# Layer 0 of a two-layer macaron block: two VectorE steps moved to GpSimd and ScalarE

## The chip, the cores and the metric

One core of a Trainium2 chip runs the whole program. The metric is the device time of one execution in microseconds (us). Engines are called by their short names: PE is TensorE (PEld its weight loads), DVE is VectorE, ACT is ScalarE, POOL is GpSimd, SP is SyncE, which issues most of the DMAs. Matrix products land in PSUM, a small memory of eight banks per partition that PE, DVE and ACT use; the kernel keeps everything else in SBUF.

## The reference

The input x is 16 sequences of 512 tokens of width 128. Two layers follow each other, each as "half an FFN, attention, half an FFN". The change touches layer 0 only:

```python
x = x + 0.5 * ffn(layernorm(x))          # FFN with fp4-quantized inputs
x = x + attn(layernorm(x))               # 16 heads of width 8, relative positions
x = x + 0.5 * ffn(layernorm(x))
# ffn:
gate = fp4_linear(x, w_gate); y = fp4_linear(x, w_up)
h = silu(gate) * y
return fp4_linear(h, w_down)
# attn:
score = q @ k + q . pe_k[dist]           # dist = clip(j - i, -64, 64) + 64
attn = softmax(score)
ctx = attn @ v + attn . pe_v[dist]
return ctx @ W_out + b_out
```

`fp4_quant_dequant` takes blocks of 16 numbers, divides by their largest magnitude over 6, rounds to a grid of eight values and multiplies back. `pe_v[dist]` differs from a constant only in a band of 64 on either side of the diagonal. Layer 1 (linear attention, and an ordinary attention with a mixture of experts) is not changed.

## The kernel before, in words

Layer 0 works through 16 sequences `b`, each in two halves of 256 queries, so 32 units. For each unit there are these streams of work, each a Python generator that yields between steps:

- `maxima` (L332) computes the scores in tiles of 128 keys by 512 columns on PE (L263, and L267 where the tile lies in the band), and DVE takes the maximum of each tile (L341).
- `main` (L358) computes the same scores once more, ACT takes the exponential (L369), PE multiplies with V into the averages `av`, and with the band's table into `rps`. ACT copies the band's result into `RV` (L403); SP writes `RV` to DRAM (L406) and reads it back in another layout into `cr` (four DMAs, L409). ACT copies the averages from PSUM into `cx` (L412).
- `fin` (L416) adds the band part `cr` to the averages `cx` (L422, two instructions a unit), transposes `cx` on PE (L430), divides (L433, L434), and multiplies with the output matrix.
- `F.half` (L107) is half an FFN for 256 tokens: layer norm (with a power on POOL, L59), quantization (DVE L70 to L78, POOL L79 and L81), transposes, and then for each `j` of two blocks of 128 tokens: PE makes the gate `g` (L121), ACT its tanh (L122), DVE forms `(tanh+1)*g` (L123), PE makes the 'up' `u` (L125), DVE multiplies the two (L126). Then the product is quantized, transposed, and multiplied with `w_down` (L139). It runs twice for each half sequence: as `head` before the attention, as `tail` behind it. That makes 128 blocks `j` in all.
- `prep` and `prepV` make q, k and v of a coming sequence.

`interleave` (L446) merges the generators by due times; in `layer0` a unit's `fin` is due from 0.45 of a unit after `main` ends, its `tail` after `fin`, and the `head` of three sequences later in the same unit. The order in which Python traces the instructions gives their priorities. From these and its own durations, the framework's planner lays out the order of the instructions on each engine ahead of time: an engine takes the instruction that the plan has ready first. On the chip each engine then runs its list strictly in that order, and waits where an input is late. Two devices bend the plan: `high_priority` (L341), and `issue_after(a.last)` in `fin` (L425), which keeps the add L422 behind the latest score maximum that was traced, in DVE's list.

Buffers that matter: PSUM tiles `mps` come from a pool of two (`pM`), shared by FFN, `prep` and `fin`; score tiles `sps` from a pool of three (`pS`), shared by `maxima` and `main`. The FFN's SBUF pool `fk` has two buffers of each name: `f_h`, `q_y`, `q_M` and so on. `cr` and `cx` have one buffer each.

Of the kernel before, what the change touches and what calls it, by code (L numbers as in the profile page):

```python
# [8 lines left out]
F32 = mybir.dt.float32  # L9
# [3 lines left out]
AF = mybir.ActivationFunctionType  # L13
ALU = mybir.AluOpType
# [3 lines left out]
I = 352  # L18
# [65 lines left out]
class FFN:  # L84
# [22 lines left out]
    def half(f, xb, half, wk, pp):  # L107

        s=f.s; nc=s.nc
        xh=xb[:,2*half:2*half+2,:]  # L110
        xn=wk.tile([128,2,128],F32,name="f_x")
        yield from s.ln_steps(xh,xn,wk,2)
        for xq in s.quant_steps(xn.rearrange("p a b -> p (a b)"),wk,128,16,"xq"): yield
        ps=pp.tile([128,512],F32,name="mps")
        for j in range(2): nc.tensor.transpose(ps[:,j*128:(j+1)*128],xq[:,j*128:(j+1)*128],s.ident)
        xqT=wk.tile([128,256],F32,name="f_x"); nc.scalar.copy(xqT,ps[:,:256]); yield
        h=wk.tile([128,2,I],F32,name="f_h")
        for j in range(2):
            t=h[:,j,:]
            g=pp.tile([128,512],F32,name="mps")  # L120
            nc.tensor.matmul(g[:,:I],xqT[:,j*128:(j+1)*128],f.wguT[:,0,:],start=True,stop=True)  # L121
            nc.scalar.activation(t,g[:,:I],AF.Tanh,scale=0.5)  # L122
            nc.vector.scalar_tensor_tensor(t,t,1.0,g[:,:I],ALU.add,ALU.mult); yield  # L123
            u=pp.tile([128,512],F32,name="mps")
            nc.tensor.matmul(u[:,:I],xqT[:,j*128:(j+1)*128],f.wguT[:,1,:],start=True,stop=True)  # L125
            nc.vector.scalar_tensor_tensor(t,u[:,:I],0.5,t,ALU.mult,ALU.mult); yield  # L126
        for hq in s.quant_steps(h.rearrange("p a b -> p (a b)"),wk,128,44,"hq"): yield
        hq=hq.rearrange("p (a b) -> p a b",a=2)
        for j in range(2):
            ps=pp.tile([128,512],F32,name="mps")  # L130
            for c in range(3):
                P=min(128,I-c*128)
                nc.tensor.transpose(ps[:P,c*128:(c+1)*128],hq[:,j,c*128:c*128+P],s.ident)
            hT=wk.tile([128,3,128],F32,name="hT",bufs=1)
            nc.scalar.copy(hT[:,0:2,:],ps[:,:256])
            nc.scalar.copy(hT[:96,2,:],ps[:96,256:384])  # L136
            for c in range(3):
                P=min(128,I-c*128)
                nc.tensor.matmul(ps[:,384:512],hT[:P,c,:],f.wdT[:P,c,:],start=(c==0),stop=(c==2),skip_group_check=True)  # L139
            nc.vector.scalar_tensor_tensor(xh[:,j,:],ps[:,384:512],0.5,xh[:,j,:],ALU.mult,ALU.add); yield  # L140
# [5 lines left out]
class Attn0:  # L146
# [103 lines left out]
    @staticmethod  # L250
    def vers(kt,half):

        return 1 if kt*128+192<half*256+256 else 0
# [3 lines left out]
    def scores(a, out, kt, half, b, BD, TQ, KS):  # L257

        nc=a.nc; blk=half*8+b
        sd=a.side(kt,blk); ib=a.inband(kt,blk)  # L260
        o4=out.rearrange("p (x g c) -> p g x c",x=8,g=4)
        for g in range(4):
            nc.tensor.matmul(o4[:,g],KS[:,sd,g*512+kt*128:g*512+(kt+1)*128],BD[:,g,:,b*32:b*32+32].rearrange("p h (x j) -> p x h j",j=4),start=(g==0),stop=(not ib and g==3),skip_group_check=True)  # L263
        if ib:
            for x in range(8):
                w0=kt*128-blk*32-x+a.OFF
                nc.tensor.matmul(out[:,x*64:x*64+64],a.ET[:,w0:w0+128],TQ[:,:,b*32+4*x:b*32+4*x+4],start=False,stop=(x==7),skip_group_check=True)  # L267
# [57 lines left out]
    def load(a, b, half):  # L325
        nc=a.nc; i=b%2
        u=(2*b+half)%3; BD=a.BD[u]; TQ=a.TQ[u]; QS=a.QS[i]
        for j in range(4):
            nc.sync.dma_start(BD[j*32:j*32+29,:,j,:],QS.rearrange("(g j) r q -> j r g q",j=4)[j][:,:,half*256:half*256+256])
            (nc.sync if b else nc.scalar).dma_start(TQ[j*32:j*32+24],a.QM[i][j][:,:,half*256:half*256+256].rearrange("h r q -> r h q"))  # L330
# [85 lines left out]
    def fin(a, b, half, X, wk, pM):  # L416

        s=a.s; nc=a.nc; cx,cr=a.pend.pop((b,half)); xb=X[b]
        def add():
            for s2 in range(2):  # L420
                o=cx.rearrange("p z (b j s x) -> p s (z b) x j",j=4,s=2,x=4)[:,s2]
                nc.vector.tensor_tensor(o,o,cr.rearrange("p (x j z b s) -> p s (z b) x j",x=4,j=4,z=4,s=2)[:,s2],ALU.add)  # L422
        if a.last is None: add()
        else:
            with s.tc.issue_after(a.last): add()  # L425
        yield
        cn=wk.tile([128,2,128],F32,name="cn")
        for t in range(2):
            ps=pM.tile([128,512],F32,name="mps")
            for z in range(4): nc.tensor.transpose(ps[:,z*128:z*128+128],cx[:,z,t*128:t*128+128],a.ident)  # L430
            p3=ps.rearrange("p (h c) -> p h c",c=32)
            rc=wk.tile([128,16],F32,name="rc")
            nc.vector.reciprocal(rc,p3[:,:,8])  # L433
            nc.vector.tensor_tensor(cn[:,t,:].rearrange("p (h d) -> p h d",d=8),p3[:,:,0:8],rc.unsqueeze(2).to_broadcast([128,16,8]),ALU.mult)  # L434
            yield
        ps=pM.tile([128,512],F32,name="mps")
        for t in range(2): nc.tensor.transpose(ps[:,t*128:t*128+128],cn[:,t,:],a.ident)
        ct=wk.tile([128,2,128],F32,name="cn").rearrange("p a b -> p (a b)"); nc.scalar.copy(ct,ps[:,:256])
        ps=pM.tile([128,512],F32,name="mps")
        for t in range(2): nc.tensor.matmul(ps[:,t*128:(t+1)*128],ct[:,t*128:(t+1)*128],a.wo,start=True,stop=True)  # L440
        xh=xb[:,2*half:2*half+2,:]
        nc.gpsimd.tensor_tensor(xh,xh,a.bo.unsqueeze(1).to_broadcast([128,2,128]),ALU.add)
        nc.vector.tensor_tensor(xh,xh,ps[:,:256].rearrange("p (a b) -> p a b",a=2),ALU.add)
        yield
# [593 lines left out]
```

## Time and profile before

| what | value |
| --- | --- |
| runs | 3627.19, 3630.62, 3651.11 us; median 3630.62 |
| the profiled execution | 3633.94 us, its span 3632.2 us |
| layer 0 | from the start to about 2050 us; steady from 300 to 1950 |
| busy over the span | PE 78%, DVE 67%, ACT 47%, POOL 23% |
| L126: 'up' times gate, DVE | 128 instructions, 64.6 us |
| L422: band part added, DVE | 64 instructions, 68.4 us |

The profile shows one execution. A group of instructions is given with its count, its busy time in us and the mean of one in ns; then the idle time of the engine just before, with what ended it. A window line gives the busy time of each engine in a stretch of the span, with the count of instructions. The line of tenths cuts the span into 40 slices of 90.8 us. A list of waits has us in total, how often, and the longest.

### The profile page before, as it was taken

Reading aid. Unit: us, or ns where it says so; the run is one execution under the profiler, and the core shown is the slowest. Engines: PE = TensorE matmul, PEld = TensorE weight load, DVE = VectorE, ACT = ScalarE, POOL = GpSimd, SP = SyncE. Lnnn points to the kernel's source line nnn. Section 1 sums busy time; section 2 is a strip of 40 time slices with the busy share of each in tenths; the row PEclk is TensorE's granted clock in tenths of the full one; section 3 lists DMA queues with packets and bytes.
Section 4 is the critical chain, followed back from the end, with each engine's and each line's share of the span. In section 5 each row is a group of like instructions: output and inputs, shape, how many; then the busy total and the mean of one; then the engine's idle time right before and its main releaser. Section 6 shows DMA issues by size and latency. Waiting matters only on the chain. (4 is left out here: it accounts for less than half of the span.)

```text
span 3632.2 us, 95259 instructions
## 1 busy us (share of the span) xinstructions
PE 2825.0 (78%) x40077; PEld 2032.3 (56%) x40077; DVE 2444.9 (67%) x6508; ACT 1693.8 (47%) x3391; POOL 838.9 (23%) x789
## 2 busy tenths in 40 slices
PE   5578989889898889888896388873788888878570
PEld 3357777667676677666775244431565555555230
DVE  5568788777887788877773467774546655655356
ACT  3145555545455454545554155533455454445242
POOL 4122222222222222222110222212112211111226
PEclk8799999999999999999998599886899989989785
DMA  3232222321223222222210111104312222121401
GB/s 105 54 91 71 57 53 59 81 63 52 65 65 77 64 50 58 76 74 62 53 33 19 32 33 36 36 33 123 90 54 73 59 63 56 36 62 36 126 17 46
DMA packets 290159, 217.23 MB, mean 60 GB/s; under 512 B 77402, under 2 KB 257476, under 8 KB 289604
## 3 DMA queue, kind: packets, MB, share of 16 engines
q1 hardware_dynamic: 284468, 207.72, 21.6%
q8 instruction: 315, 5.16, 0.6%
q10 hardware_dynamic: 5264, 3.43, 0.4%
q14 instruction: 112, 0.92, 0.1%
HBM read 110.28 MB, written 100.78 MB: 58 GB/s over the span
## 5 line engine op out<-in xcount | busy, mean ns | idle before, releaser
L341 DVE TRANSPOSE_TENSOR_REDUCE mx<-sps 128x16 f32<-128x512 f32 x1024 | 702.5, 701 | 261.7 <-PE sps L263 137.2
L263 PE MATMUL sps<-a_BD,a_KS 128*128 128x128 f16 x8192 | 736.4, 222 | 136.2 <-DVE mx L341 65.6
L369 ACT ACTIVATE PT<-sps 128x512 f32<-128x512 f32 x1024 | 576.4, 599 | 433.8 <-PE sps L267 238.1
L263 PEld LDWEIGHTS <-a_KS 128*128 128x128 f16 x8192 | 546.1, 98 | 296.4 <-issue 260.0
L59 POOL TENSOR_TENSOR ln_rs<-ln_ve,negh 128x4 f32<-128x4 f32 (+1 forms) x192 | 176.9, 930 | 855.1 <-DVE ln_ve L58 760.6
L267 PE MATMUL sps<-a_TQ,a_ET 128*128 128x64 f16 x7168 | 370.3, 195 | 0.0
L721 DVE SCALAR_TENSOR_TENSOR moe<-mps,oh,moe 128x128 f32<-128x128 f32 x896 | 289.8, 341 | 110.7 <-PE mps L719 96.5
L79 POOL TENSOR_TENSOR q_M<-q_y,q_M 128x704 f32<-128x704 f32 (+2 forms) x129 | 157.0, 1218 | 784.6 <-DVE q_y L78 658.6
L719 PE MATMUL mps<-f_W,T 128*128 128x512 f32 x512 | 297.1, 701 | 24.8 <-DVE moe L721 20.0
L267 PEld LDWEIGHTS <-a_ET 128*128 128x128 f16 x7168 | 311.2, 99 | 2.3 <-issue 1.9
L274 PE MATMUL av<-PT,a_V 128*32 128x256 f32 x3840 | 251.9, 387 | 0.0
L894 DVE TENSOR_TENSOR a_at<-pp,a_cm 128x1024 f32<-128x1024 f32 x128 | 154.3, 1214 | 79.6 <-PE pp L892 78.6
L892 PE MATMUL pp<-a_F 64*128 64x128 f32 x2048 | 169.8, 306 | 41.4 <-DVE a_at L894 30.2
L892 PEld LDWEIGHTS pp<-a_F 64*128 64x128 f32 x2048 | 143.3, 206 | 93.0 <-DVE a_at L894 36.9
L719 PEld LDWEIGHTS mps<-f_W,T 128*128 128x128 f32 x512 | 102.7, 222 | 125.0 <-issue 75.3
L274 PEld LDWEIGHTS av<-PT,a_V 128*32 128x32 f32 x3840 | 121.4, 111 | 68.7 <-issue 5.0
L874 ACT ACTIVATE a_F<-pp 128x1024 f32<-128x1024 f32 x128 | 127.0, 1025 | 46.8 <-PE pp L872 40.5
L62 ACT ACTIVATE xn<-xn,ln_mr,ln_rs 128x128 f32<-128x128 f32 x256 | 103.6, 481 | 95.5 <-DVE ln_mr L60 75.2
L274 PE MATMUL rps<-PT,a_TV 128*32 128x64 f32 x6912 | 134.5, 222 | 4.6 <-issue 4.4
L139 PE MATMUL mps<-wdT,hT 128*128 128x128 f32 (+1 forms) x768 | 126.9, 301 | 5.6 <-ACT hT L136 4.0
L673 ACT COPY f_PT<-St 32x512 f32<-32x512 f32 x128 | 78.7, 615 | 106.0 <-DVE St L672 99.9
L872 PE MATMUL pp<-a_QK,a_PK 128*128 128x512 f16 x256 | 82.7, 413 | 54.4 <-DMA a_QK<-a1d 26.6
(342 smaller groups left out, 5330.2 us busy)
## 6 DMA issues: line engine op xcount, KB each, us to landing
QM<-a_HM SPq DMA_DIRECT2D x180, 128.0 KB
a_TQ<-QM SPq DMA_DIRECT2D x120, 192.0 KB
RD<-RV SPq DMA_DIRECT2D x32, 512.0 KB
a_KS<-KSd SPq DMA_DIRECT2D x128, 96.0 KB
a_QK<-a1d SPq DMA_DIRECT2D x128, 96.0 KB
xn<-X SPq DMA_DIRECT2D x32, 256.0 KB
a1d<-a_hi SPq DMA_DIRECT2D x64, 128.0 KB
a_BD<-QS SPq DMA_DIRECT2D x128, 58.0 KB
```

The lines of the kernel that those rows point to most:

```text
L59: nc.gpsimd.tensor_tensor(rs,ve,s.negh[:,:n],ALU.pow); yield
L79: nc.gpsimd.tensor_tensor(M[:P],y[:P],M[:P],ALU.subtract)
L263: nc.tensor.matmul(o4[:,g],KS[:,sd,g*512+kt*128:g*512+(kt+1)*128],BD[:,g,:,b*32:b*32+32].rearrange("p h (x j) -> p x h j",j=4),start=(g==0 ...
L267: nc.tensor.matmul(out[:,x*64:x*64+64],a.ET[:,w0:w0+128],TQ[:,:,b*32+4*x:b*32+4*x+4],start=False,stop=(x==7),skip_group_check=True)
L274: for p,q in mms[1:]: a.nc.tensor.matmul(*p,**q)
L341: with a.s.tc.high_priority(): r=nc.vector.tensor_reduce(mx[:,kt,:,bb],ps.rearrange("p (i c) -> p i c",c=32),axis=AX.X,op=ALU.max,apply_tr ...
L369: nc.scalar.activation(pt[:,:,bb*32:bb*32+32].rearrange("p h (x j) -> p x h j",j=4),ps.rearrange("p (x h j) -> p x h j",x=8,j=4),AF.Exp)
L719: nc.tensor.matmul(ps,yT[:,j*128:(j+1)*128],a.W[:,e2*4:e2*4+4,:],start=True,stop=True)
L721: nc.vector.scalar_tensor_tensor(moe[:,j,:],ps[:,e*128:(e+1)*128],oh[:,j,e2*4+e:e2*4+e+1],moe[:,j,:],ALU.mult,ALU.add)
L874: nc.scalar.activation(f,ps,AF.Relu)
L892: nc.tensor.matmul(ps[:,hh,bs],f[hh*64:hh*64+64,1,bs],f[hh*64:hh*64+64,0,bs],start=True,stop=True)
L894: nc.vector.tensor_tensor(k,ps.rearrange("p h (b q) -> p (h b) q",b=4),a.cm.unsqueeze(1).to_broadcast([128,8,128]),ALU.mult)
```

## The change

Two edits in layer 0. In the FFN, ACT copies `u` from PSUM into an SBUF tile `v`, with the factor 0.5, and POOL multiplies `t` by `v`; DVE did both in one instruction. The tile `v` takes a buffer of the name `q_y`, which the quantization uses as well. In `fin` the two adds go to POOL, and the order behind `a.last` is dropped.

```diff
@@ FFN.half
             nc.vector.scalar_tensor_tensor(t,t,1.0,g[:,:I],ALU.add,ALU.mult); yield
             u=pp.tile([128,512],F32,name="mps")
             nc.tensor.matmul(u[:,:I],xqT[:,j*128:(j+1)*128],f.wguT[:,1,:],start=True,stop=True)
-            nc.vector.scalar_tensor_tensor(t,u[:,:I],0.5,t,ALU.mult,ALU.mult); yield
+            v=wk.tile([128,704],F32,name="q_y")[:,:I]; nc.scalar.activation(v,u[:,:I],AF.Copy,scale=0.5); nc.gpsimd.tensor_tensor(t,t,v,ALU.mult); yield
@@ Attn0.fin
         def add():
             for s2 in range(2):
                 o=cx.rearrange("p z (b j s x) -> p s (z b) x j",j=4,s=2,x=4)[:,s2]
-                nc.vector.tensor_tensor(o,o,cr.rearrange("p (x j z b s) -> p s (z b) x j",x=4,j=4,z=4,s=2)[:,s2],ALU.add)
-        if a.last is None: add()
-        else:
-            with s.tc.issue_after(a.last): add()
+                nc.gpsimd.tensor_tensor(o,o,cr.rearrange("p (x j z b s) -> p s (z b) x j",x=4,j=4,z=4,s=2)[:,s2],ALU.add)
+        add()
         yield
```

## Prediction

> **What bounds the kernel now.** I read the page's tenths first, then stages of the span, then short windows inside layer 0, then the waits, then the groups by shape. The change touches layer 0 alone, which ends near 2050 us, so the shares of the whole span say little.
>
> ```profile
> PE   5578989889898889888896388873788888878570
> DVE  5568788777887788877773467774546655655356
> POOL 4122222222222222222110222212112211111226
> ```
>
> Slices 4 to 21 are layer 0's steady part: PE at 80 to 90%, DVE at 70 to 80%, POOL at 20%. By stages (PE, PEld, DVE, ACT, POOL busy, then clock, DMA share and GB/s):
>
> ```profile
> 300.00:1950.00 1650.00, 1455.67 (x26315) 1152.24 (x26308) 1282.15 (x2837) 841.24 (x1845) 366.65 (x344) 0.97 0.24 61
> 1950.00:2050.00 100.00, 51.20 (x672) 35.69 (x670) 41.89 (x108) 25.70 (x61) 23.79 (x28) 0.69 0.07 16
> ```
>
> No engine is full there: PE 88%, DVE 78%, ACT 51%, POOL 22%. Windows of 4 us show that the average hides two regimes:
>
> ```profile
> 1020.00:1024.00 4.00, 4.00 (x126) 2.94 (x119) 1.38 (x3) 2.90 (x8) 0.00 (x0) 1.00 0.16 37
> 1032.00:1036.00 4.00, 2.65 (x27) 1.32 (x24) 4.00 (x11) 1.55 (x3) 0.00 (x0) 1.00 0.57 155
> 1044.00:1048.00 4.00, 2.16 (x67) 1.62 (x55) 4.00 (x11) 1.41 (x6) 0.39 (x1) 1.00 0.24 45
> 1088.00:1092.00 4.00, 2.25 (x25) 1.97 (x27) 3.97 (x9) 1.47 (x3) 2.54 (x2) 1.00 0.00 0
> ```
>
> In the first, PE is full and DVE idles; in the others DVE is full and PE stands a third to half of the time. So DVE sets the pace in part of each unit. Cut into 4 us windows, 300 to 1950 us has 243 windows (972 us) with DVE 80% busy or more. PE idles 134.6 us in them (14%), and 60 us (9%) in the other 680. The waits say the same:
>
> ```profile
> PE sps L263 <- DVE mx L341: 48.9, 68, 3.9
> PE sps L263 <- ACT PT L369: 33.0, 77, 2.6
> PE mps L430 <- DVE cx L422: 12.5, 4, 9.9
> PE mps L133 <- POOL q_M L81: 4.5, 11, 0.9
> DVE ln_st L55 <- DMA x<-in_L_attn_x_dram: 45.5, 11, 5.2
> POOL qklo L144 <- DMA QS<-qklo: 84.8, 8, 13.4
> ```
>
> PE waits for DVE most, for ACT second, for POOL hardly. The last two lines are needed for a rival: transfers land later than the plan has them.
>
> **The change part by part.** Groups by shape:
>
> ```profile
> L422 DVE TENSOR_TENSOR cx<-cx,a_cr 128x512 f32<-128x512 f32 x64 | 68.4, 1119 | 20.7 <-DMA a_cr<-RD 20.7
> L126 DVE SCALAR_TENSOR_TENSOR f_h<-mps,f_h 128x352 f32<-128x352 f32 x128 | 64.6, 504 | 5.9 <-PE mps L125 5.4
> L99 ACT COPY wguT<-mps 128x352 f32<-128x352 f32 x2 | 0.8, 456 | 1.2 <-PE mps L98 1.2
> L79 POOL TENSOR_TENSOR q_M<-q_y,q_M 128x256 f32<-128x256 f32 x64 | 46.5, 727 | 150.7 <-DVE q_y L78 137.8 <-PE sps L263 10.2 <-DMA a_BD<-QS 1.4
> L669 POOL TENSOR_TENSOR S<-S,src 128x512 f32<-128x512 f32 x32 | 33.5, 1047 | 170.4 <-DVE src L668 122.3 <-ACT a_xT L830 44.1 <-DVE lg L701 1.5
> L298 POOL COPY a_HM<-qklo 128x512 f16<-128x512 f16 x16 | 27.9, 1744 | 1.0
> ```
>
> *Taken off DVE.* 133 us in all; the windows of L126 and L422 alone put 53.3 + 64.2 = 117.4 us of it between 300 and 1950, and 100.8 us of that in the 243 packed windows.
>
> *Given back by blocking.* A DVE instruction can stand behind POOL:
>
> ```profile
> 1080.16 0.18 DVE L71 TENSOR_SCALAR hq_sc<-hq_sc 128x44 f32<-128x44 f32 x1
> 1089.23 1.39 POOL L81 TENSOR_TENSOR q_M<-q_M,hq_sc 128x704 f32<-128x704 f32 x1
> 1089.68 0.98 DVE L71 TENSOR_SCALAR hq_sc<-hq_sc 128x44 f32<-128x44 f32 x1
> ```
>
> The same L71 took 0.18 us alone and 0.98 us when it began under L81. Over 300 to 1950, DVE instructions that overlapped POOL took some 40 us more than the medians of their forms without overlap; POOL was busy 367 us, so 0.11 us per us. New POOL work there: 106 products of 0.95 us (between L79's 727 ns for 256 columns and 1704 for 704, by columns) and 60 adds. The add reads and writes in steps of 32 and 256 bytes, which no POOL tensor_tensor here does. Its bounds: 1.05 us (L669, 512 columns contiguous) and 3.6 us (L687's 1267 ns times 1744/612, the strided copy L298 over the contiguous copy L902). I take L298's 1.74, the one strided row with 512 columns. That is 101 + 104 = 205 us, and 0.11 times it is 22 us back on DVE. Net relief 95 us, in the packed windows 0.84 of it: 80. Bounds: 0 and 45 us (double) back.
>
> The Trainium skill, SBUF — State Buffer, § Who interferes with whom, says that POOL shares a port pair with DVE as an exclusive lock: whichever starts first blocks the other for its whole instruction, if the DVE one has two SBUF inputs or runs in a two-port mode. By that rule L126, whose one input is PSUM, never met POOL, and its replacement does; L71's two rows agree. Were each of the 166 new POOL instructions to block one DVE instruction for half of itself, the sum would have 103 us back instead of 22, and the gain would be gone.
>
> The GPSIMD Engine Reference, § 7, says that reading SBUF with steps over 8 bytes costs about half more per element. With L687's 1.27 us that makes an estimate of 1.9 us an add, 122 us for 64 against my 111; no run here shows it, and § 4.1 of that page advises against elementwise work on this engine at all.
>
> *What the relief is worth.* Were the packed windows to fall to the others' 8.8% PE idle, they would shorten by x with 134.6 - x = 0.088 (972 - x), so x = 54. That is what taking all 100.8 us away could return before PE binds; I take 54 * 80/101 = **-42 us**. Ends: 0 and -80.
>
> *ACT's copies.* 128 of 0.456 us (L99, same shape): 58 us, ACT from 51% to 54% of the stretch. Each stands in ACT's list among the exponentials L369, and has to wait for PE's L125 and for a free `q_y` buffer; behind it stand L369, and PE waits for those through three `sps` buffers. ACT cost PE 33.0 us in 841 us of work; 50 us more make +2, and as much twice over for the waits at the head of its list: **+6**. Ends: 0 and +35 (doubling that row). `u`'s `mps` buffer is now freed by ACT instead of DVE, at about the same length, so no term.
>
> *POOL's results.* PE's L430 and DVE's L70 now wait for POOL. In POOL's list the products and adds stand in front of L59, L79, L81, L144 and L442. Nearest row: PE lost 4.5 us to 53 results of L81, 0.085 each; 106 products and 30 adds at that make **+12**. Ends: 0, and 5 us a unit (two adds of 3.6 in place of 1.12, all seen by PE) for 30 units, +150. Between the read of `cr` (L409) and DVE's add lie 8 to 22 us in the trace, which cover a longer add; if the planner moves L430 up, that cover goes.
>
> *Start and end.* Where nothing lies beside it (first heads, last two tails), a block pays 0.46 + 0.95 - 0.50 = 0.9 us and one more handover; six such blocks, 5 us, and the last add 2 * (1.74 - 1.12) = 1.2: **+7** with rounding up. Ends +2 and +15.
>
> *Nothing:* no DMA is moved or added; SP's list is as before, and `cr` is read again 40 us or more after the add. Layer 1 is untouched.
>
> Sum: -42 + 6 + 12 + 7 = -17 us on the profiled 3633.9, so **3617 us**. That execution lies 3.3 us above the median.
>
> **The rivals.**
>
> *Slower: POOL stands at the head of its list for `cr`.* Without the order behind `a.last`, the plan puts the add where it has `cr` landed; POOL is idle then and will take it at once. For: loads land later than planned (DVE waited 45.5/11 = 4.1 us for x each time, POOL 10.6 us for QS). While POOL stands, L79, L81, L59 and the new products stand behind it, DVE's L70 and L60 wait for those, and PE for DVE. Price: 4.1 us a unit, 30 units, 123 us; three quarters seen by PE, 92. In place of the +12: 3634 - 42 + 6 + 7 + 92 = 3697. It decides (over 1% slower) from 2.2 us a unit on. Against: DVE's add itself waited for `cr` only twice.
>
> *Faster: DVE sets the packed stretches alone.* The net relief comes through whole: 3634 - 80 + 6 + 7 = 3567. For: PE's biggest wait is on DVE. Against: PE's 88%.
>
> *The relief does nothing:* PE and DVE only trade places in the wait for each other, and the costs stay: 3634 + 25 = 3659.
>
> **How the numbers follow.** Forecast 0.33 (own range 3590 to 3650), slower rival 0.30, faster 0.23, no relief 0.14. One per cent, about what a measurement of this kernel can tell from no change, is 36 us: below 3594 lie the faster rival and 0.04 of the forecast, 0.27; above 3667 the slower rival and 0.05 of the no-relief case, 0.35; 0.38 between. The range takes in both rivals' values: 3560 to 3715, with some 0.1 left out on each side.
>
> **What would show it.** DVE in 300 to 1950 from 78% to 72%, POOL to 35%; the packed windows fewer. Adds of 1.74 us, products of 0.95, copies of 0.46. Small DVE instructions (L58, L60, L71) lengthened more often. Slower rival: POOL's wait for `a_cr<-RD` appears at 2 us a unit or more, and PE or DVE waits for POOL lines. What would make it wrong: an add over 3 us, ACT waiting long for a `q_y` buffer, or a new order of the whole plan.

## The result and the profile after

| | before | after |
| --- | --- | --- |
| median of the runs | 3632.1 us (3627.2 to 3651.1) | 3983.9 us (3977.2 to 3995.3) |
| span of the profiled execution | 3632.2 us | 3993.6 us |
| mean granted TensorE clock | 0.900 | 0.861 |

The ratio is 1.096, 95% interval 1.091 to 1.101: slower by 352 us, outside the range. Line numbers behind the adds of `fin` are lower by 2 in the kernel after (L430 is L428 there, L475 is L473). Units are counted from 0, so an odd unit is the second half of a sequence.

To see where the time went I cut each span at the end of the second L412 of a unit (its averages are copied), and at the last L140. A pair is two units, one sequence. "x" is DVE's idle time at L55 in the waits of over 1.5 us for x; "cr" is the idle time ahead of the adds L422 in all.

| us | start to unit 2 | unit 2 to 24 (a pair) | 24 to 31 | rest of layer 0 | layer 1 | x | cr |
| --- | --- | --- | --- | --- | --- | --- | --- |
| before | 364.3 | 1273.1 (115.7) | 342.0 | 65.6 | 1587.4 | 45.5 | 20.7 |
| after | 384.8 | 1557.1 (141.6) | 396.3 | 70.0 | 1585.4 | 75.9 | 466.3 |

Layer 1 is as before; the loss is 26 us in every pair, and more where the pipeline fills and drains. The page's tenths of after (slices of 99.8 us):

```profile
PE   5677787778778778777877755888278887887661
DVE  5566576567657557655755524777555665555446
POOL 5223223223323322322321122222211211111135
```

PE is at 70 to 80% where it was at 80 to 90%, DVE at 50 to 70%, and POOL at 20 to 30%: no engine is nearer its limit, all stand more. The window that holds about the same 26,300 matmuls as 300 to 1950 did before is now 2000 us long:

```profile
300.00:2300.00 2000.00, 1535.60 (x26293) 1205.92 (x26285) 1246.83 (x2678) 881.18 (x1948) 587.97 (x511) 0.88 0.20 50
```

The groups of the new work:

```profile
L422 POOL TENSOR_TENSOR cx<-cx,a_cr 128x512 f32<-128x512 f32 x64 | 128.0, 2037 | 466.3 <-DMA a_cr<-RD 442.0 <-ACT PT L369 19.9 <-ACT hT L136 4.5
L126 POOL TENSOR_TENSOR f_h<-f_h,q_y 128x352 f32<-128x352 f32 x128 | 124.3, 971 | 393.4 <-ACT q_y L126 339.7 <-DVE f_h L123 37.4 <-DVE mx L341 15.9
L126 ACT ACTIVATE q_y<-mps 128x352 f32<-128x352 f32 x128 | 59.6, 466 | 100.1 <-PE mps L125 92.7 <-POOL q_M L79 3.3 <-POOL ln_rs L59 0.2
```

An add takes 2.04 us (1.74 taken), a product 0.97 (0.95), a copy 0.466 (0.456): the durations were nearly right. What was not is the 442 us that POOL stands ahead of the adds for `cr`. The waits between 300 and 2300 show who stands with it:

```profile
POOL cx L422 <- DMA a_cr<-RD: 408.7, 23, 31.7
DVE ln_mr L60 <- POOL ln_rs L59: 195.4, 48, 18.0
PE sps L263 <- DVE mx L341: 155.2, 86, 15.5
PE mps L115 <- POOL q_M L81: 144.8, 10, 17.5
DVE ln_st L55 <- DMA x<-in_L_attn_x_dram: 75.9, 11, 9.3
PE mps L428 <- POOL cx L422: 50.7, 5, 18.5
```

In the steady part of before, PE's wait for DVE's L341 was 48.9 us, PE's for L81 4.5 us (at L133), and DVE's for L59 next to nothing:

```profile
DVE ln_mr L60 <- POOL ln_rs L59: 1.7, 4, 0.9
```

One odd unit of after (unit 11) shows the chain. Timeline of POOL: start, duration, and in brackets the idle time before with what ended it.

```profile
1005.88 1.38 POOL L59 TENSOR_TENSOR ln_rs<-ln_ve,negh 128x2 f32<-128x2 f32 x2 [14.00 <-DVE ln_ve L58]
1032.04 3.88 POOL L422 TENSOR_TENSOR cx<-cx,a_cr 128x512 f32<-128x512 f32 x2 [24.78 <-DMA a_cr<-RD]
1035.87 0.72 POOL L79 TENSOR_TENSOR q_M<-q_y,q_M 128x256 f32<-128x256 f32 x1
1036.55 1.02 POOL L59 TENSOR_TENSOR ln_rs<-ln_ve,negh 128x4 f32<-128x4 f32 x1
```

POOL is free at 1007.3, and the next instruction in its list is the add, for which `cr` lands at 1032. Behind it stands an L59 that only now can run; DVE has stood for that one:

```profile
1037.60 0.68 DVE L60 SCALAR_TENSOR_TENSOR ln_mr<-ln_mv,ln_rs 128x4 f32<-128x4 f32 x1 [14.54 <-POOL ln_rs L59]
```

SP's own list in the same place. `stream` has `loads` fetch the tables from which the next unit's scores are made: the keys into `a_KS` (L315, once in two units), the queries into `a_BD` and `a_TQ` (L329, L330, four each). The last copy into `RV` (ACT, L403) ends at 1011.1; its write to `RD` is issued at 1018.4, 7 us later, behind the last of these loads in SP's list, and the read back into `cr` 9.5 us after that:

```profile
1014.92 3.41 SPq L330 DMA_DIRECT2D a_TQ<-QM  x1
1018.43 0.72 SPq L406 DMA_DIRECT2D RD<-RV  x1
1027.98 1.37 SPq L409 DMA_DIRECT2D a_cr<-RD  x4
```

And windows of 4 us, columns as in the prediction:

```profile
1020.00:1024.00 4.00, 3.90 (x70) 2.62 (x68) 2.04 (x3) 1.73 (x4) 0.00 (x0) 1.00 0.25 74
1024.00:1028.00 4.00, 0.83 (x16) 0.65 (x12) 0.00 (x0) 0.00 (x0) 0.00 (x0) 0.95 0.19 74
1028.00:1032.00 4.00, 0.00 (x0) 0.00 (x0) 0.00 (x0) 0.00 (x0) 0.00 (x0) 0.50 0.15 33
1032.00:1036.00 4.00, 0.00 (x0) 0.00 (x0) 0.00 (x0) 0.00 (x0) 3.96 (x3) 0.50 0.01 2
1040.00:1044.00 4.00, 4.00 (x34) 3.25 (x33) 0.27 (x1) 2.53 (x6) 0.79 (x2) 0.50 0.00 0
```

From 1025 to 1032 no engine works, and then until 1036 POOL alone, on the add. The early add gains nothing for it: PE's L428, which uses it, starts at 1059.9, 24 us after the add ended. In the steady part odd units wait 24 to 26 us, even ones 3 to 6.

### The profile page after: what moved, and what is told of

Read it like the earlier page. It is cut to its first block, busy times and chain, and to the rows that moved or that the text cites. A ratio compares the mean times of both kernels' runs of the same rounds, so it can differ in the third digit from the quotient of the medians.

```text
span 3993.6 us, 95395 instructions
## 1 busy us (share of the span) xinstructions
PE 2906.8 (73%) x40077; PEld 2089.8 (52%) x40077; DVE 2396.3 (60%) x6316; ACT 1745.4 (44%) x3519; POOL 1091.3 (27%) x981
## 5 line engine op out<-in xcount | busy, mean ns | idle before, releaser
L263 PE MATMUL sps<-a_BD,a_KS 128*128 128x128 f16 x8192 | 771.4, 228 | 232.6 <-DVE mx L341 169.0
L341 DVE TRANSPOSE_TENSOR_REDUCE mx<-sps 128x16 f32<-128x512 f32 x1024 | 700.0, 699 | 326.8 <-PE sps L267 211.4
L263 PEld LDWEIGHTS <-a_KS 128*128 128x128 f16 x8192 | 573.2, 101 | 405.1 <-issue 369.8
L267 PE MATMUL sps<-a_TQ,a_ET 128*128 128x64 f16 x7168 | 387.0, 199 | 1.7 <-issue 1.5
L59 POOL TENSOR_TENSOR ln_rs<-ln_ve,negh 128x4 f32<-128x4 f32 (+1 forms) x192 | 176.2, 927 | 670.0 <-DVE ln_ve L58 629.6
L267 PEld LDWEIGHTS <-a_ET 128*128 128x128 f16 x7168 | 329.1, 102 | 3.0 <-issue 2.2
L274 PE MATMUL av<-PT,a_V 128*32 128x256 f32 x3840 | 276.8, 415 | 0.0
L422 POOL TENSOR_TENSOR cx<-cx,a_cr 128x512 f32<-128x512 f32 x64 | 128.0, 2037 | 466.3 <-DMA a_cr<-RD 442.0
L126 POOL TENSOR_TENSOR f_h<-f_h,q_y 128x352 f32<-128x352 f32 x128 | 124.3, 971 | 393.4 <-ACT q_y L126 339.7
L60 DVE SCALAR_TENSOR_TENSOR ln_mr<-ln_mv,ln_rs 128x4 f32<-128x4 f32 (+1 forms) x192 | 66.4, 347 | 251.0 <-POOL ln_rs L59 249.6
L274 PEld LDWEIGHTS av<-PT,a_V 128*32 128x32 f32 x3840 | 130.0, 118 | 80.6 <-issue 25.9
L872 ACT ACTIVATE a_F<-pp 128x1024 f32<-128x1024 f32 x128 | 126.6, 1025 | 44.3 <-PE pp L870 38.1
L115 PE MATMUL mps<-ident,q_M 128*128 128x128 f32 x128 | 29.7, 347 | 157.6 <-POOL q_M L81 156.2
```

Source lines behind the costliest of these rows:

```text
L59: nc.gpsimd.tensor_tensor(rs,ve,s.negh[:,:n],ALU.pow); yield
L274: for p,q in mms[1:]: a.nc.tensor.matmul(*p,**q)
L341: with a.s.tc.high_priority(): r=nc.vector.tensor_reduce(mx[:,kt,:,bb],ps.rearrange("p (i c) -> p i c",c=32),axis=AX.X,op=ALU.max,apply_tr ...
L422: nc.gpsimd.tensor_tensor(o,o,cr.rearrange("p (x j z b s) -> p s (z b) x j",x=4,j=4,z=4,s=2)[:,s2],ALU.add)
```

## The experiments

Three theories stood at first. *Place* (theory 1 in the expectations): the add lost its place behind `a.last`, so the engine that has it stands at the head of its list for `cr`. *FFN* (theory 2): ACT's copies, POOL's products and the shared `q_y` buffers cost it. *GpSimd* (theory 3): the adds and products are slow there, or block DVE. Each ratio is to the kernel before on the same chip.

| run | ratio, 95% interval | a pair, us | x | cr |
| --- | --- | --- | --- | --- |
| e1_ffn_only | 1.027 (1.025 to 1.029) | 123.6 | 95.8 | 20.7 |
| e2_add_only | 1.088 (1.085 to 1.090) | 138.0 | 79.4 | 413.5 |
| e3_add_ordered | 1.065 (1.063 to 1.067) | 133.2 | 53.9 | 331.2 |
| e4_dve_unordered | 1.072 (1.069 to 1.075) | 133.1 | 17.6 | 353.5 |
| e5_no_dma | 1.032 (1.030 to 1.035) | 125.8 | 81.3 | 120.0 |
| e6_ffn_noload | 1.002 (1.000 to 1.004) | 115.5 | 0 | 20.9 |
| e7_before_noload | 0.993 (0.990 to 0.996) | 114.7 | 0 | 20.9 |
| e8_act_dve | 1.024 (1.022 to 1.027) | 124.5 | 95.2 | 21.1 |
| e9_add_late | 1.057 (1.054 to 1.059) | 130.5 | 177.9 | 160.5 |
| e10_ffn_xact | 1.020 (1.017 to 1.023) | 123.3 | 93.9 | 21.0 |
| e11_late_noload | 1.060 (1.057 to 1.063) | 132.9 | 0 | 416.7 |
| e12_before_xact | 1.006 (1.004 to 1.009) | 119.2 | 80.9 | 20.8 |
| e13_ffn_xfirst | 1.004 (1.002 to 1.006) | 116.6 | 22.8 | 20.8 |
| e14_rd_first | 1.079 (1.073 to 1.085) | 136.3 | 43.6 | 652.2 |
| e15_noprod_noload | 0.984 (0.981 to 0.988) | 111.7 | 0 | 20.4 |
| e18_before_xkfirst | 0.988 (0.986 to 0.990) | 113.5 | 30.0 | 21.4 |
| e19_half_xfirst | 0.998 (0.996 to 1.000) | 115.5 | 47.5 | 21.3 |
| e20_half_xkfirst | 0.988 (0.986 to 0.990) | 113.2 | 34.1 | 22.0 |

The ratios are of the whole program. Layer 1, which no run edits, takes 1573 to 1606 us in the profiled executions, so part of a small difference need not come from the edit. In layer 0 alone, one execution of each, e1 is 92 us longer than before, e6 12 us longer than e7, e13 20 us longer than before, e18 28 us shorter than before, and e15 46 us shorter than e7.

### The parts alone: e1, e2

e1 is the change's first edit alone, e2 its second alone.

> The FFN edit alone: the band add stays on VectorE behind a.last. Theory 1 (GpSimd stands at the head of its list for the transfer into cr, because the add lost its place in the order): the loss is gone, 3590 to 3660 us. Theory 2 (the FFN's ScalarE copies, GpSimd products and the shared q_y buffers cost it): the loss stays, 3900 us or more. Theory 3 (GpSimd has too much strided and port-blocking work): between, since 128 us of adds go and 124 us of products stay: some 3800.

> The band add alone on GpSimd, without its place in the order; the FFN as before. Theory 1: most of the loss, 3880 to 4000 us, with GpSimd waiting over 300 us for a_cr<-RD. Theory 2: 3610 to 3660. Theory 3: some 3800.

The add alone costs 8.8% of 3642, 319 us; the FFN edit alone 2.7%, 99 us. That sums to 418 against the change's 352: the two losses overlap. Neither run came out as one theory alone would have it; two causes were to be found, not one.

### The add: e4, e5, e3

e4 leaves the add on DVE and drops only the order:

```diff
-        if a.last is None: add()
-        else:
-            with s.tc.issue_after(a.last): add()
+        add()
```

> The kernel before, with one thing undone: the add of the band part stays on VectorE but is no longer ordered behind the last row maximum, so it stands in VectorE's list where the planner puts it. If the loss of the change came from the lost place (the engine stands at the head of its list for the transfer of cr), VectorE stands now, and everything behind it: 3800 to 4000 us, with over 200 us of waits ahead of L422 for a_cr. If it came from GpSimd as such (a slow strided add, the shared work of the two engines), this kernel is as before: 3620 to 3660 us, with under 40 us of such waits.

The waits of e4 between 300 and 2300:

```profile
DVE cx L422 <- DMA a_cr<-RD: 346.6, 31, 22.2
```

7.2% slower with nothing moved to GpSimd. The place in the list does most of it, on either engine: e2, which differs from e4 only in the engine, loses 8.8%.

e5 is the whole change, but the adds read a constant table in `cr`'s layout, so that no transfer is waited for (the band part is left out):

```diff
-                nc.gpsimd.tensor_tensor(o,o,cr.rearrange(...)[:,s2],ALU.add)
+                nc.gpsimd.tensor_tensor(o,o,a.TV[0].rearrange("p x v d -> p (x v d)")[:,:1024].rearrange(...)[:,s2],ALU.add)
```

> Both edits as in the changed kernel, but the adds read a constant tile in the place of cr, so that they wait for no transfer (this leaves the band part out of the averages; cr is still written and read back). Theory 1: 3580 to 3660 us, though the adds stand where the plan likes. Theories 2 and 3: 3900 or more, since the adds take as long.

1.032 instead of 1.096: without the transfer, the same 64 adds (2.13 us each here) cost 0.5% beyond e1's 1.027, though POOL still waits 120 us, now for ACT's copy of `cx`. So adds that are slow on GpSimd, or block DVE, are not what costs 7 to 9%.

e3 gives the add a place again: behind the latest traced POOL instruction (L59, L81 or a product).

```diff
-        add()
+        with s.tc.issue_after(s.lastp): add()
```

> Both edits, and the two adds on GpSimd are queued behind the latest GpSimd instruction of the FFN or of a layer norm that was traced before them. Work and engines are those of the changed kernel; only the place in GpSimd's list differs. Theory 1: 3580 to 3660 us, GpSimd's wait for a_cr<-RD under 50 us. Theories 2 and 3: still 3900 or more.

It takes a third of the loss away, not all, and misses what was expected: from unit 7 on POOL's waits are 5.5 us in even and 17 in odd units, and now PE stands as well, since its list has the transposes right behind the add:

```profile
PE mps L428 <- POOL cx L422: 243.2, 24, 19.2
```

### Can the add be put late enough? e9, e11, e14

e9 is e3 without the FFN edit, with `fin` due at (.8,.95) of a unit instead of (.45,.9). e11 is e9 without the loads of x from sequence 5 on (`xload` begins with `if b>=5: X[b]=X[b-5]; return`). e14 is e2 with `with tc.issue_after(s.lastr): A.load(u//2,u%2)` in `loads`, from unit 4 on, where `s.lastr` is the last L406. First e9's edit:

```diff
-        W=dict(part=0,V=(.6,.7),fin=(.45,.9),prep=(0,.7),tail=1.0,head=(-.1,1))
+        W=dict(part=0,V=(.6,.7),fin=(.8,.95),prep=(0,.7),tail=1.0,head=(-.1,1))
```

> The band add alone on GpSimd, as in e2, but the adds are due later (0.8 of a unit behind the end of main in place of 0.45) and queued behind the latest GpSimd instruction of the FFN or a layer norm traced before them. In e3, with 0.45, GpSimd still stood 5.5 and 17 us a unit for cr; 0.35 of a unit is some 20 us. Theory 1 (the wait for the transfer, and nothing else of the add, is the loss): GpSimd's wait for a_cr<-RD under 60 us and 3610 to 3690 us, against e2's 3960. Theory 3 (strided adds on GpSimd are costly in themselves): 3750 or more with the wait gone.

> Both ways in which the add on GpSimd was seen to lose time are taken away at once, without the FFN edit: the add on GpSimd is ordered behind GpSimd's other work and its step is given out later (.8 to .95 of a unit instead of .45 to .9), and sequences 5 to 15 reuse the x of five earlier instead of loading it (so the output is of other data there). If standing for cr and the late x are the whole cost of the move, 3620 to 3690 us beside 3624 for the kernel before with the same loads left out. If the strided add on GpSimd costs by itself or through the port that it shares, 3750 us or more.

> The add alone on GpSimd, unordered (3960 us so far, 414 us of waits ahead of the adds), with the table loads of the next unit ordered behind the last RD transfer (L406) that was issued. If the 25 us that GpSimd stands in odd units come from RD queued behind those loads, they fall to 10 to 16 us, the waits in all to 220 to 320 us and the time to 3800 to 3900 us. If they come only from the early place of the add in GpSimd's list, waits and time stay: over 380 us, over 3930 us.

In e9 the waits for `cr` in units 4 to 24 are 0 to 3 us, as wanted, but the time lies where theory 3 had it. The trace gives another reason: the tail, due after `fin`, is later too, and DVE's wait for x grows from 45.5 to 178 us. The loss changes its place, and the run does not decide what the adds cost by themselves. e11 was to add the two repairs. Its time is in theory 3's range as well, but it is inconclusive: with the loads gone the plan came out otherwise and POOL waits 20 us in odd units again (366 us between 300 and 2300). e14 missed. `RD` is issued 3 us after `cx` is copied in odd units instead of 6 in e2, but the plan moved the add up as well: from unit 7 on POOL waits 24 to 30 us in odd units and 16 to 17 in even ones (13 and 7 in e2). The time is still lower than e2's, as the wait for x is. In its odd units from 7 on the write to `RD` follows the last copy into `RV` within 0 to 2 us, where it took 5 us in e2, but from that write to the read into `cr` it takes 13 to 16 us instead of 10. So by the trace of after `RD`'s place in SP's list is 7 of the odd units' 25 us, and what moving it could gain is open. In all of these runs, but for the steady part of e9, POOL's list reaches the add before the round trip from `RV` to `cr` has ended.

### The FFN edit: e8, e6, e7

e6 is e1, and e7 the kernel before, without the loads of x from sequence 5 on (edit as in e11). e8 keeps ACT's copy and multiplies on DVE. The expectations weigh theory A, a later tail and so a later store and load of x; theory B, POOL's products, which block DVE or come late; and theory C, ACT's copies, which stand before the exponentials. e8's edit:

```diff
-            nc.vector.scalar_tensor_tensor(t,u[:,:I],0.5,t,ALU.mult,ALU.mult); yield
+            v=wk.tile([128,704],F32,name="q_y")[:,:I]; nc.scalar.activation(v,u[:,:I],AF.Copy,scale=0.5); nc.vector.tensor_tensor(t,t,v,ALU.mult); yield
```

> Of the FFN edit only ScalarE's copy into a q_y buffer; VectorE multiplies from SBUF, where GpSimd did; the band add as before. Theory C: most of e1's 98 us stay, 3700 to 3740. Theory B: they go, 3630 to 3660. Theory A: in between by how much later the tail still is, 3650 to 3690.

> The FFN edit alone, as in e1, and sequences 5 to 15 are not loaded: each goes on from the old contents of the tile that sequence b-5 left (this leaves out those loads). It takes away VectorE's stand at L55 for the load of x, 8.7 us a sequence in e1 against 4.3 before. Theory A (the FFN edit costs by a later tail, a later store and so a later load of x): 3640 us, 40 to 50 above e7. Theory B (GpSimd's products cost by blocking VectorE and by coming late) and theory C (ScalarE's copies cost by standing before the exponentials): still about 100 us above e7, 3690 or more.

> The kernel before, with sequences 5 to 15 not loaded, as in e6 (this leaves out those loads). The reference for e6. VectorE's 45 us at L55 go; by theory A most of them come out as time, 3590 to 3605 us; if other work covers that stand, 3630.

e8 loses 2.4%, with the product on DVE, so the product on GpSimd is not needed for a loss of this size. Without the loads the FFN edit's loss falls from 99 us to 28 (3651.5 against 3623.7), and to 0.8 us a pair in the steady part. Most of the loss is thus in the loads of x. What is left is little, so neither theory B nor C is the main cause. Sequence b's x goes into the tile of sequence b-5, when the tail's store of that one (L486) is done. SP in e1:

```profile
1154.28 0.78 SPq L486 DMA_DIRECT2D X<-x  x1
1155.16 1.01 SPq L330 DMA_DIRECT2D a_TQ<-QM  x1
1156.22 0.80 SPq L329 DMA_DIRECT2D a_BD<-QS  x1
1157.08 3.22 SPq L330 DMA_DIRECT2D a_TQ<-QM  x1
1160.39 0.69 SPq L475 DMA_DIRECT2D x<-in_L_attn_x_dram  x1
```

and DVE there:

```profile
1166.24 1.07 DVE L55 BATCH_NORM_STATS2 ln_st<-x 128x6 f32<-128x128 f32 x5 [8.69 <-DMA x<-in_L_attn_x_dram]
```

The same place in the kernel before, SP and DVE:

```profile
1106.01 0.39 SPq L486 DMA_DIRECT2D X<-x  x1
1109.90 0.39 SPq L475 DMA_DIRECT2D x<-in_L_attn_x_dram  x1
```

```profile
1113.66 1.06 DVE L55 BATCH_NORM_STATS2 ln_st<-x 128x6 f32<-128x128 f32 x5 [4.74 <-DMA x<-in_L_attn_x_dram]
```

From store to L55 it took 7.7 us before and 12.0 in e1, and so it is in all eleven sequences: from store to load 2.2 to 3.9 us before and 5.9 to 6.4 in e1, from load to L55 3.1 to 5.0 and 5.7 to 6.2. Before, SP issues nothing between the two; in e1 it issues three table loads there. The tail ends a little later: the store is issued 48 to 51 us after the last copy of `cx` in an even unit instead of 45, and so it and the load fall among the next unit's table loads.

### Place in SyncE's list, or the transfers beside it? e10, e12, e13

e10 is e1, and e12 the kernel before, with the loads of x issued by ACT:

```diff
-            nc.sync.dma_start(t,tok(src,b))
+            (nc.scalar if b>4 else nc.sync).dma_start(t,tok(src,b))
```

> The FFN edit alone (1.027 of before so far), with the loads of x from sequence 5 on issued by ScalarE instead of SyncE, so that they no longer stand behind the table loads (L329, L330) in SyncE's list. If the FFN edit loses because x is issued behind those loads, VectorE's wait for x (L55) falls from 96 us to under 50 and the time to 3650 to 3690 us (ratio 1.002 to 1.013; ScalarE may stand some us a sequence for the store that frees the tile). If the loss is in ScalarE's extra copies themselves, or in the later tail apart from x, the time stays at 3720 us or more.

> The kernel before with the loads of x from sequence 5 on issued by ScalarE instead of SyncE: the control for the same edit made with the FFN part. VectorE's wait for x is 45 us in the kernel before. If the wait is for the place in SyncE's list, 10 to 25 us of it go and the time is 3615 to 3635 us (ratio 0.993 to 0.998); if it is for the store that frees the tile and the transfer itself, nothing changes, and ScalarE standing at the head of its list for that store may cost 0 to 40 us (ratio 1.0 to 1.011).

e10 missed: the wait for x is as long. ACT's timeline there says why:

```profile
1158.77 0.37 ACTq L475 DMA_DIRECT2D x<-in_L_attn_x_dram  x1
1159.18 1.06 ACT L412 COPY cx<-av 128x512 f32<-128x512 f32 x1 [5.15 <-DMA X<-x]
```

ACT was ready, and stood 5.15 us for the store, which SP had issued at 1152.55 with L330 right behind it: 6.2 us until the load could go, where it was 3.9. From the load to L55 it took 6.3 us more, where it was 3.8. The place in SP's list is thus not the whole of it: the store and the load take longer with the tables' transfers beside them, whoever issues them. The Trainium skill says the same of the engines behind the queues (DMA: Bandwidth & Descriptors, § Issuing engines are not separate DMA queues): transfers from any issuer run on the same sixteen engines and interleave. In e12 the load follows the store as closely as before (2.1 to 4.2 us), but SP, which no longer stands for the store, issues tables in that time, and from the load to L55 it takes 5.5 to 7.7 us instead of 3.1 to 5.0: x is waited for 81 us.

e13 is e1 with the unit's tables (not the keys, L315) ordered behind x:

```diff
+            r=nc.sync.dma_start(t,tok(src,b)); s.lastx=r.ins
...
-                A.load(u//2,u%2)
+                with tc.issue_after(s.lastx): A.load(u//2,u%2)
```

> The FFN edit alone, with the table loads of the next unit (L329, L330) ordered behind the last load of x that was issued, so that the store of the finished half, then x, go to the transfer engines ahead of them, as in the kernel before. If the FFN edit loses because its later tail brings the store and x among the table loads, VectorE's wait for x (L55) goes from 96 to 35 to 55 us and the time to 3640 to 3690 us (ratio 1.000 to 1.013). If the tail's lateness itself is the loss, 3715 us or more (ratio over 1.02), whatever the wait for x is.

```profile
1114.78 0.39 SPq L487 DMA_DIRECT2D X<-x  x1
1117.38 0.39 SPq L475 DMA_DIRECT2D x<-in_L_attn_x_dram  x1
1117.83 0.36 SPq L329 DMA_DIRECT2D a_BD<-QS  x1
1118.28 1.10 SPq L330 DMA_DIRECT2D a_TQ<-QM  x1
```

Store to load 2.6 us, the wait for x 22.8 us in all, and the time at 1.004. The store is as late as in e1 (47 to 50 us after the even unit's `cx`), so the later tail alone does not cost it. So most of the FFN edit's 99 us were the store and the load of x among the table loads: 71 by taking the loads away (e6 against e7), 84 by moving the tables (e13); in layer 0 alone it is 81 and 73 of 92. The 84 may hold a gain that the kernel before would have had too: its control, this order without the FFN edit, was not run, and e18 below, which moves the key tables as well, is faster than before.

### Is there a relief of VectorE? e15, e19, e18, e20

e15 is e7 with the multiplication left out altogether (L126 becomes a bare `yield`). e19 is e13 with only the first of a half's two products handed over (`if j==0:` as in the change, else as before). e18 is the kernel before with all table loads ordered behind x, e20 is e18 with the first product handed over. e18's edit, beside the `s.lastx` of e13:

```diff
-                if u%2==0: A.loadK(u//2)
-                A.load(u//2,u%2)
+                with tc.issue_after(s.lastx):
+                    if u%2==0: A.loadK(u//2)
+                    A.load(u//2,u%2)
```

> The kernel before without the multiplication by FFN's up in layer 0 (L126 left out altogether, the matmul ahead of it kept), and with sequences 5 to 15 reusing earlier x instead of loading it; to be compared with 3624 us of the kernel before with the same loads left out. VectorE loses 128 instructions of 0.5 us and nobody gets them. By the relief booked in the prediction (42 of 117 us in the steady part, about a third) 64 us less on VectorE would save some 20 us: 3595 to 3610 us, 112.5 to 113.5 us a pair of units instead of 114.7. If VectorE's time was not the limit: 3615 to 3635 us, over 114 us a pair.

> The FFN edit for the first of a half's two products only (the second is multiplied on VectorE as before), with the table loads ordered behind x as in the run before it that had both products (ratio 1.0041). If the relief is lost because the quantisation of the half waits for the second product, half of the relief stays and nothing is late: 3610 to 3630 us (ratio 0.992 to 0.998). If the hand-over as such costs what it brings, 3635 to 3650 us (0.998 to 1.003).

> The kernel before with the key tables (L315) and the unit's tables (L329, L330) ordered behind the last load of x that was issued. VectorE's wait for x is 45.5 us in the kernel before; leaving the loads out saved 0.7%. If the transfers in flight beside x set that wait, it falls to 20 to 35 us and the time by 5 to 20 us (ratio 0.994 to 0.999); if the tables, now later, are waited for instead, 1.000 to 1.01.

> The two before it together: the first product only on ScalarE and GpSimd, and key tables and unit tables ordered behind x. If both gains are real and add, 3600 to 3625 us (ratio 0.988 to 0.997); if neither is, 3635 to 3660 us (0.998 to 1.006).

Taking 64.6 us off DVE and giving them to nobody saves 31 to 41 us (ratios 0.984 and 0.993 on two chips; medians 3582.5 and 3623.7), 3.0 a pair, more than the 20 expected. It also takes a step out of the FFN's chain, so how much of that is DVE's time alone was not separated. Given to ACT and POOL the products bring nothing (e6: 115.5 a pair against 114.7). e19 shows part of the reason: with the first product alone the time is at 0.998, with both (e13) at 1.004, though x is waited for longer (47.5 us against 22.8). So handing over the second, which the quantization L70 waits for at once, costs about 0.6%; whether by that wait or by its copy on ACT was not tested. In e18 the order of SP's list alone, with nothing moved, gives 0.988, 43 us faster than before: a version that beats both kernels. That is more than the 5 to 20 us expected, and more than DVE's wait for x, which falls by 15.5 us only; where the rest comes from is open. Handing over the first product on top of it (e20) changes nothing that can be measured.

## Why the prediction was wrong

**The step that failed most is the price of POOL standing for `cr`.** The forecast's sum had +12 for those who wait for POOL's results, and nothing for POOL's own wait. The prediction had the mechanism as its slower rival, at 92 us, with 4.1 us a unit taken from waits for *x*, and 0.30 of chance; the add alone cost 319 us (e2). POOL stands 15 us a unit in the steady part of after (24 to 26 in odd, 3 to 6 in even units), and 466 us in all. The trace of before held a better row: SP's own L406 and L409. ACT, SP and DVE in its unit 13:

```profile
993.51 1.99 ACT L412 COPY cx<-av 128x512 f32<-128x512 f32 x2 [0.44 <-PE av L274]
1010.11 0.72 SPq L406 DMA_DIRECT2D RD<-RV  x1
1020.05 1.36 SPq L409 DMA_DIRECT2D a_cr<-RD  x4
1028.59 2.09 DVE L422 TENSOR_TENSOR cx<-cx,a_cr 128x512 f32<-128x512 f32 x2
```

`cx` was copied at 995.5 and the last part of `cr` was issued at 1021.4, 26 us later. In units 2 to 24 it is 26 to 29 us in odd units and 0 to 2 in even ones, 14 a unit on average. An add that its list puts close behind `cx` stands about that long; the prediction priced it from how late other loads were. Its own rule (30 units, three quarters of the wait seen by PE) would have made 315 us of 14 us a unit. That this meets e2's 319 is partly luck, as the three quarters were a guess.

**"Against: DVE's add itself waited for `cr` only twice"** was no evidence: it waited seldom because `a.last` put it 6 to 23 us behind the issue of the last read of `cr` (units 2 to 24). The row showed the order at work, which the change takes away. The same holds for the 8 to 22 us that "cover a longer add": they were made by that order. e4 shows its worth, 7.2%.

**"SP's list is as before" was wrong**, and a term that was put at nothing was most of the FFN edit's 99 us (71 by e6 and e7). No DMA is moved in the code, but the plan lays SP's list out anew, and a tail that ends a little later put the store and x behind L329 and L330.

**The relief.** Booked at -42 us for 133 us. e15 shows 31 to 41 for 64.6 us, so the step's time on DVE and its place in the FFN's chain together do bind, by more than was taken. But no hand-over that was run keeps any of it: with both products the steady part is 0.8 us a pair longer (e6 against e7), with the first alone in e18's order nothing changes (e20).

**Given back by blocking: 22 us.** DVE's busy time fell by 48.6 us (2444.9 to 2396.3) where 133 were taken off, so 84 went into longer instructions: L74 of 704 columns from 952 to 1142 ns, L76 of 256 columns from 300 to 564. L71, which the prediction named as a sign, went the other way with 44 columns, from 310 to 151 ns. The rule of the Trainium skill (SBUF — State Buffer, § Who interferes with whom), which the prediction put at 103 us, was nearer in size than the 0.11 row. It isn't shown to be the cause: in e15, with no work added on POOL, DVE's busy time fell by only 26 us of 64.6.

**Copies, durations, ends.** The durations held within 3% but for the add (2.04 for 1.74 us). The copies' own cost was not measured apart from the rest; start to unit 2 grew by 20 us where +7 was booked for start and end together, most of it with the add (e2 19, e1 -1).

**Slips in the working.** None of them decides. 100.8 of 117.4 us is 0.86, not 0.84. The slower rival passes 1% from 2.9 us a unit on if three quarters are seen by PE; 2.2 holds without that share. And `cr` is read again 31 us after the add of an odd unit, not 40 or more.

## What to carry to other kernels

Where an instruction waits for a transfer, its price on another engine is not its duration but its place in that engine's list: work out from the trace when its input lands and what stands behind it there, and keep an explicit order if the old place had one. An edit that moves no DMA can still shift a store into the midst of other transfers; look for what is issued next to it. An order of the transfers alone was worth 1.2% here, and the two moves of vector work nothing.

## What the runs showed of the hardware

When PE stands, its clock falls too, and the work behind pays. In after the granted clock is 0.50 in the windows of a stand (1028 to 1036 above) and still 0.50 from 1040 to 1044, where PE is busy again; four matmuls of L263 took 0.63 us there and 0.39 us from 1045 on. The mean from 300 to 2300 is 0.88 where it was 0.97, and PE is busy 1536 us for the 26,300 matmuls that took 1456. So up to 80 of the 352 us can be that.

An issue of L330, the same load each time, kept SP for 0.3 to 3.7 us. In after the four of unit 11 with their L329, one right behind the other, held back what was listed behind by 15 us (1003.4 to 1018.4).
